# Attention stage: shift products moved ahead of the maxima's products, a turn moved ahead of the output projection

## The chip, the cores and the metric

The kernel runs on one core of a Trainium2 chip. A core has a matrix engine (TensorE, "PE" in the profile, with its weight loads shown apart as "PEld"), VectorE ("DVE"), ScalarE ("ACT"), GpSimd ("POOL") and a queue that issues transfers (SyncE, "SP"). Matrix products land in an accumulator memory (PSUM), which this kernel uses as eight banks, and VectorE or ScalarE read them from there. The metric is the device time of one execution in microseconds: the median of three executions was 3641.82 us (3641.27 to 3644.77).

## The reference, cut to what matters

The input has 16 images of 64 x 64 positions with 128 features. A group normalisation and a two-dimensional recurrence run first, then Nystroem attention over the 4096 tokens of each image (8 heads of 16, 64 landmarks), then a recurrent feed-forward part. The change lies in the attention, of which this is the core:

```
q, k, v = jnp.split(xn @ w_qkv, 3, axis=-1)            # to 8 heads of 16
q_l = q.reshape(b, h, m, l, dh).mean(axis=3)           # 64 landmarks
k_l = k.reshape(b, h, m, l, dh).mean(axis=3)
attn1 = softmax(einsum('bhid,bhjd->bhij', q, k_l))
attn2 = softmax(einsum('bhid,bhjd->bhij', q_l, k_l))
attn3 = softmax(einsum('bhid,bhjd->bhij', q_l, k))
out = attn1 @ moore_penrose_pinv(attn2) @ (attn3 @ v)  # + convolution of v
out = out @ w_out + b_out
```

Both large softmaxes subtract a maximum. In the kernel a maximum is split into three bf16 parts, and a small bf16 product with ones adds the negated maximum into the bank in which the fp32 score products then accumulate; ScalarE takes the exponential from there.

## The kernel before, in words

Attention works on groups of 512 tokens, 8 groups to an image, 128 groups in all. It is a software pipeline over steps: in step `s` the group `new` is projected to keys, values and queries; `mid`, eight steps older (one image back), gets its weights over the landmarks' queries (attn3) and its product with the values; and `first`, `cur`, `third`, `fourth`, `fifth`, `sixth`, some sixteen steps older, go through attn1, the output projection and the feed-forward product. Steps 0 to 7 run `first_step`, 8 to 14 `second_step`, 15 to 127 `step`, and the rest `last_step`. A step that begins an image (`q == 0`, called `start` in the code) also finishes the older image's sums (`gather`, `spread_values`) and makes its shift (`turn_split`).

The order of the work on PE, DVE, ACT and POOL is written out by hand: each engine takes its instructions in the order in which the step calls them. Each name `bank0` to `bank5` and `pair` (two banks) has one buffer, so a new tile of a name waits until the last reader of the tile before it is done.

The parts of a step that the change touches, in order:

- `project_queries` (L997) writes bank 5 with `new`'s queries, and `keep_queries` (L1001) copies them out on ScalarE at L1003.
- `greatest` (L1020) writes the landmark scores of `new` to banks 0 to 3, four row groups of 32 partitions each, and `keep_greatest` (L1026) reduces the four banks to maxima on VectorE, in `step` in the order 3, 2, 1, 0.
- `weigh` (L1048) takes banks 4, 5 and `pair`; it writes the bf16 shift products of `mid` (L1054) and accumulates the fp32 score products (L1060) on them. `weights` (L1066) takes the exponentials on ScalarE, in tile `at_e`, which has one buffer; `add_weights` (L1089) sums them on GpSimd.
- `part_top` (L1143) splits the maxima of `first` on GpSimd, `turn_top` (L1152) turns them on PE into bank 2, and `keep_top` (L1157) copies them out on ScalarE.
- `output` (L1205) projects `third` into bank 3; `keep_sum` (L1210) reads it on VectorE.
- After them come `turn_output` (L970, L960), `attend` (L1175), `convolve`, `divide` (which uses bank 2), `feed` (bank 3, L1238), `turn_rows`, `attend_values`, `soften` and, in the next step, `compare` and the projections.

Of the kernel before, what the change touches and what calls it, by code (L numbers as in the profile page):

```python
# [14 lines left out]
P = 128  # L15
# [830 lines left out]
def attention(nc, tc, t1, gamma, beta, wqkv, ident, mhalf, fixed, xp, rows, qm, km, pinvT, vd, t2, wx, wx_stats, out, ahead):  # L846
# [14 lines left out]
    C = 4  # L861
# [4 lines left out]
    BF = mybir.dt.bfloat16  # L866
    with ExitStack() as ctx:
# [7 lines left out]
        def bank(k, shape, dtype=F32):  # L875
            return ps.tile(shape, dtype, tag=f"bank{k}", name=f"at_bank{k}")

        def banks(*ks):
            return [bank(k, [P, GC]) for k in ks]
# [60 lines left out]
        def carry_factors(gr):  # L940
            gr.nbt = nb = sm.tile([P, 2, C], F32, tag="nb", name="at_nb")
            nc.gpsimd.tensor_tensor(nb[:, 1], gr.T[:, :, F], gr.T[:, :, F + 2], ALU.mult)
            nc.gpsimd.tensor_scalar(nb[:, 0], gr.T[:, :, F + 2], 1.0, None, ALU.add)

        def carry(gr, c, eng):
            x, scale, bias = gr.T[:, c, 0:F], gr.nbt[:, 0, c : c + 1], gr.nbt[:, 1, c : c + 1]
            if eng is nc.scalar:
                nc.scalar.activation(x, x, AF.Identity, bias=bias, scale=scale)
            else:
                eng.tensor_scalar(x, x, scale, bias, ALU.mult, ALU.add)  # L950
# [54 lines left out]
        def turn_split(im):  # L1005
            r = bank(3, [P, P])
            nc.tensor.transpose(r, split.rearrange("p n s -> p (n s)"), ident)
            im.minus = wk.tile([P, P], BF, tag="minus", name="at_minus3")
            nc.scalar.copy(im.minus, r)
# [10 lines left out]
        def greatest(gr):  # L1020

            gr.s = banks(0, 1, 2, 3)
            for n in range(NP):
                nc.tensor.matmul(gr.s[n], gr.im.qm[quarter(n)], gr.KT[quarter(n)], start=True, stop=True)  # L1024
# [20 lines left out]
            im.sums = sm.tile([P, P], F32, tag="sums", name="at_sums")  # L1045
            im.total = wk.tile([P, NP, P], F32, tag="total", name="at_total", bufs=2)

        def weigh(gr, ks=(4, 5)):  # L1048

            both = pair()  # L1050
            s = (*banks(*ks), both[:, 0], both[:, 1])
            im = gr.im
            for n in range(NP):
                nc.tensor.matmul(  # L1054
                    s[n].rearrange("p (c m) -> p c m", c=C), ones_b[n * W2 : n * W2 + 3, :],
                    im.minus[n * W2 : n * W2 + 3, None, :].to_broadcast([3, C, P]), start=True, stop=False,
                )
            for c in range(C):
                for n in range(NP):
                    nc.tensor.matmul(  # L1060
                        s[n][:, c * P : (c + 1) * P], gr.KT[quarter(n), c * P : (c + 1) * P],
                        im.qm[quarter(n)], start=False, stop=(c == C - 1),
                    )
            gr.s = s

        def weights(gr, order=range(NP)):  # L1066
            gr.e = wk.tile([P, NP, C, P], F32, tag="e", name="at_e")
# [75 lines left out]
        def part_top(gr):  # L1143

            gr.top = top = tops[gr.g % 2]
            mx = gr.mx.rearrange("p n c j -> p n j c")
            nc.gpsimd.tensor_copy(top[:, :, 0:2], mx)
            nc.gpsimd.tensor_tensor(mx, mx, top[:, :, 0:2], ALU.subtract)
            nc.gpsimd.tensor_copy(top[:, :, 2:4], mx)
            nc.gpsimd.tensor_tensor(top[:, :, 4:6], mx, top[:, :, 2:4], ALU.subtract)  # L1150

        def turn_top(gr):  # L1152
            gr.pt = bank(2, [P, C, P], BF)
            for c in range(C):
                nc.tensor.transpose(gr.pt[:, c, :], gr.top[:, :, :, c].rearrange("p n s -> p (n s)"), ident_b)

# [74 lines left out]
        def normalise(gr):  # L1231
            gr.z = wk.tile([P, C, F], F32, tag="z", name="at_z")
            for c in range(C):
                nc.scalar.activation(  # L1234
                    gr.z[:, c, :], gr.u[:, c, :], AF.Identity, bias=gr.nb[:, c : c + 1], scale=gr.r3[:, c : c + 1]
                )
# [48 lines left out]
        def second_step(s):  # L1285
            new, after, mid, was = group(s), group(s + 1), group(s - Q), group(s - Q - 1)
            project_keys(new)
            if not was:
                sums(mid.im)
            project_values(new)  # L1290
            if was:
                attend_values(was, 3)
            keep_keys(new)
            keep_projected(new)
            if was:
                keep_values(was)
            turn_rows(after)
            keep_rows(after)
            project_queries(new)
            keep_queries(new)  # L1300
            if not was:
                turn_split(mid.im)
            greatest(new)
            weigh(mid)
            keep_greatest(new, range(NP))
            weights(mid)
            add_weights(mid, (3, 1, 0, 2), mid.g == 0)
            fetch(s)

        def last_step(s):  # L1310
            b, q = divmod(s, Q)
            mid, was = group(s - Q), group(s - Q - 1)
            first, cur, third, fourth, fifth = (group(s - 2 * Q + d) for d in (1, 0, -1, -2, -3))
            start = q == 0
            if s == (B + 1) * Q:
                kvs.close()
            if not cur:
                idle_products(nc, banks(5)[0], ident, wqkv, 384, 384)
                if fourth:
                    normalise(fourth)  # L1320
            if first:
                compare(first)
            if cur:
                softened(cur)
            if start and mid:
                measure_feed(group(s - 2 * Q - 4))
                normalise(fifth)
                turn_output(fifth)
                keep_output(fifth)
                sums(mid.im)  # L1330
                measure(fourth)
                factors(fourth)
                turn_split(mid.im)
            if first:
                topmost(first)
                carry_factors(first)
                carry(first, 2, nc.gpsimd)
            if start and was:
                gather(was.im)
            if first:  # L1340
                part_top(first)
                carry(first, 3, nc.gpsimd)
            if third:
                output(third, 0)
                keep_sum(third)
                measure(third, (0, 1))
            if not cur:
                idle_products(nc, banks(5)[0], ident, wqkv, 384, 384)
            if fifth:
                feed(fifth, 1)  # L1350
            if start and was:
                spread_values(was.im)
            if mid:
                weigh(mid, (2, 3))
                weights(mid, (2, 3, 1, 0))
            if fifth:
                keep_feed(fifth)
            if cur and fourth:
                normalise(fourth)
            if cur:  # L1360
                attend(cur)
            if mid:
                add_weights(mid, (3, 1, 0), mid.g == 0)
            if cur:
                convolve(cur, pair())
                divide(cur, 3)
            if first:
                turn_top(first)
                keep_top(first)
            if cur:  # L1370
                add_convolved(cur)
            if mid:
                attend_values(mid)
                keep_values(mid)
            if fourth:
                turn_output(fourth, 4)
                keep_output(fourth)
            if first:
                carry(first, 0, nc.scalar)
                carry(first, 1, nc.scalar)  # L1380
                soften(first)
            if cur:
                turn_attended(cur)
            if third:
                measure(third, (2, 3))
                factors(third)
            if first:
                carry_bias(first)
            if fifth:
                measure_feed(fifth)  # L1390
            if mid:
                add_weights(mid, (2,), eng=nc.vector)
            fetch(s)
            ahead(s - B * Q)

        def step(s):
# [3 lines left out]
            start = q == 0  # L1400
# [26 lines left out]
                turn_split(mid.im)  # L1427
            if fifth:
                normalise(fifth)
            greatest(new)  # L1430
            if first:
                carry_factors(first)
                carry(first, 2, nc.gpsimd)
            weigh(mid)
            keep_greatest(new)
            if first:
                part_top(first)
            if third:
                output(third)
            weights(mid)  # L1440
            if first:
                carry(first, 3, nc.gpsimd)
            if start and was:
                spread_values(was.im)
            if first:
                turn_top(first)
            if fifth:
                turn_output(fifth)
# [384 lines left out]
```

## Time and profile before

| what | value |
|---|---|
| median of three executions | 3641.82 us |
| the profiled execution, own time | 3638.97 us |
| its span, first to last instruction | 3637.4 us |
| PE, DVE, ACT, POOL busy | 96%, 82%, 69%, 68% of the span |
| first attention steps begin at about | 1615 us |
| a regular step of `step` | 12.77 us |
| a step of `step` that begins an image | 15.79 us |
| steps 10 to 13 (`second_step`) | about 7.55 us |

The page of the profile gives busy time by engine and by group of instructions. A group's row names the line, the engine, the tiles written and read, the shape, the count, the busy time and mean duration, and then the idle time of that engine just before these instructions with what ended it. The timeline lists instructions in order of time: start, duration, engine, line, tiles, count, and in square brackets idle time before and what ended it. "Busy" on PE counts a product until its modelled end, so products that overlap show no gap even where the array waited for a moment. The weight loads have rows of their own. An fp32 product runs as two passes, so eight MATMUL records of L1024 are four products.

### The profile page before, as it was taken

How to read it: one execution, taken by the hardware profiler on the slowest of the kernel's cores; microseconds unless marked ns; L12 is line 12 of the kernel's file. 1: busy time of each engine (PE TensorE's matmuls, PEld its weight loads, DVE VectorE, ACT ScalarE, POOL GpSimd, SP SyncE). 2: the span in 40 equal slices, each digit the busy share in tenths (PEclk: the TensorE clock that was granted, in tenths of full speed). 3: DMA queues.
4: the chain of work that ended last, by engine and by line, in shares of the span. 5: the costliest groups of instructions: out<-in, count | busy, mean ns of one | idle time of the engine just before them, and what ended most of it. 6: DMA issues, size and time to landing. Idle time of an engine off the chain costs nothing. (4 is left out here: it accounts for less than half of the span.)

```text
span 3637.4 us, 99065 instructions
## 1 busy us (share of the span) xinstructions
PE 3503.6 (96%) x36874; PEld 2372.5 (65%) x36874; DVE 2987.7 (82%) x7005; ACT 2499.6 (69%) x5126; POOL 2487.0 (68%) x3843
## 2 busy tenths in 40 slices
PE   7899999999999998999999999999999999997988
PEld 6666665545567666975666666666666666654777
DVE  8699999998889887544888888888888888888665
ACT  0466556666667666345788888888888888876787
POOL 1577877777788885325777777777777777785223
PEclk9999999999999999999999999999999999999999
DMA  9223332333333321033777777777676777667799
GB/s 349 76 75 79 81 84 81 83 83 86 87 86 85 80 77 36 4 74 85 165 174 186 166 165 164 163 167 163 161 162 162 162 166 164 157 143 187 199 273 183
DMA packets 834182, 484.04 MB, mean 133 GB/s; under 512 B 304672, under 2 KB 800672, under 8 KB 833696
## 3 DMA queue, kind: packets, MB, share of 16 engines
q1 hardware_dynamic: 814026, 442.55, 47.7%
q0 software_dynamic: 17728, 34.61, 5.3%
q8 instruction: 294, 4.82, 0.6%
q14 instruction: 192, 1.57, 0.1%
q10 hardware_dynamic: 1942, 0.50, 0.1%
HBM read 239.21 MB, written 238.29 MB: 131 GB/s over the span
## 5 line engine op out<-in xcount | busy, mean ns | idle before, releaser
L1096 POOL TENSOR_TENSOR at_total<-at_total,at_e 128x512 f32<-128x512 f32 x472 | 601.4, 1274 | 238.1 <-ACT at_e L1069 218.5
L290 ACT ACTIVATE ls_g<-ls_z,ls_b 128x304 f32<-128x304 f32 (+26 forms) x950 | 493.4, 545 | 222.8 <-PE ls_z L288 190.8
L283 PE MATMUL ls_z<-ls_xn,ls_w 128*128 128x432 f32 (+28 forms) x1700 | 587.4, 493 | 1.5 <-POOL ls_xn L275 1.2
L283 PEld LDWEIGHTS ls_z<-ls_xn,ls_w 128*128 128x128 f32 x1700 | 310.6, 191 | 189.6 <-issue 98.9
L288 PE MATMUL ls_z<-ls_hsum,ls_u 128*128 128x304 f32 (+26 forms) x1140 | 367.9, 459 | 0.0
L1028 DVE TENSOR_REDUCE at_mxq<-at_bank 128x1 f32<-128x512 f32 x512 | 317.7, 682 | 52.8 <-PE at_bank L1024 52.8
L323 POOL TENSOR_TENSOR ls_tt<-ls_ve,mhalf 128x8 f32<-128x8 f32 (+2 forms) x190 | 312.8, 1646 | 18.3 <-DVE ls_ve L322 2.0
L288 PEld LDWEIGHTS ls_z<-ls_hsum,ls_u 128*128 128x128 f32 x1140 | 210.1, 192 | 128.3 <-issue 78.3
L1173 ACT ACTIVATE at_eT<-at_bank 128x512 f32<-128x512 f32 x512 | 264.3, 603 | 41.4 <-PE at_bank L1168 40.8
L406 ACT ACTIVATE ls_g<-ls_cell 128x304 f32<-128x304 f32 (+26 forms) x190 | 93.2, 491 | 268.4 <-DVE ls_cell L405 268.4
L288 PE MATMUL ls_z<-ls_h,ls_u 128*128 128x304 f32 (+26 forms) x760 | 255.4, 459 | 12.3 <-DVE ls_h L410 12.3
L402 POOL TENSOR_TENSOR ls_g<-ls_g,ls_cell 128x304 f32<-128x304 f32 (+26 forms) x190 | 180.4, 949 | 126.6 <-ACT ls_g L290 115.8
L340 ACT ACTIVATE ls_tt<-ls_tt,ls_nb 128x128 f32<-128x128 f32 (+9 forms) x632 | 261.0, 478 | 4.3 <-POOL ls_tt L323 3.4
L275 POOL TENSOR_TENSOR ls_xn<-ls_xn,grstd 128x272 f32<-128x272 f32 (+40 forms) x186 | 209.8, 1128 | 75.1 <-DVE ls_xn L270 66.7
L1139 DVE TENSOR_REDUCE at_cmx<-at_bank 128x8 f32<-128x512 f32 x256 | 175.5, 685 | 104.0 <-PE at_pair L1131 102.4
L1244 ACT COPY at_fx<-at_bank 128x512 f32<-128x512 f32 x128 | 134.1, 1048 | 143.6 <-PE at_bank L1240 138.0
L1615 DVE SCALAR_TENSOR_TENSOR rc_y<-rc_w,rc_scale,rc_z 128x256 f32<-128x256 f32 x344 | 154.5, 480 | 86.2 <-PE rc_z L1602 84.4
L1234 ACT ACTIVATE at_z<-at_u,at_nb,at_r 128x128 f32<-128x128 f32 x512 | 209.6, 484 | 4.6 <-POOL at_nb L1229 4.5
L288 PEld LDWEIGHTS ls_z<-ls_h,ls_u 128*128 128x128 f32 x760 | 141.1, 191 | 106.8 <-issue 52.5
L1596 POOL DMA_DIRECT2D out_dram<-rc_tt x64 | 77.4, 1209 | 168.2 <-ACT rc_tt L1593 147.8
L1189 DVE STREAM_TRANSPOSE at_t<-at_bank 128x512 f32<-128x512 f32 x256 | 167.9, 694 | 28.4 <-PE at_bank L1180 27.3
L1602 PE MATMUL rc_z<-rc_y,rc_vT 128*128 128x256 f32 x688 | 172.9, 392 | 12.5 <-ACT rc_y L1623 11.8
(283 smaller groups left out, 9809.6 us busy)
## 6 DMA issues: line engine op xcount, KB each, us to landing
at_win<-vd SPq DMA_DIRECT2D x256, 256.0 KB
t<-ls_tt SPq DMA_DIRECT2D x392, 130.0 KB
at_T<-t SPq DMA_DIRECT2D x128, 264.0 KB
gs_xb<-in_x_dram SPq DMA_DIRECT2D x64, 512.0 KB
at_xh<-t SPq DMA_DIRECT2D x128, 256.0 KB
vd<-at_v SPq DMA_DIRECT2D x128, 256.0 KB
t<-at_u SPq DMA_DIRECT2D x128, 256.0 KB
out_dram<-at_u SPq DMA_DIRECT2D x128, 256.0 KB
```

The source lines that it names most:

```text
L275: eng.tensor_tensor(a, a, norm(v, grstd), ALU.mult)
L283: nc.tensor.matmul(v.z[g][:, : v.total], wt[g], v.xn[:, : v.total], start=True, stop=True)
L288: nc.tensor.matmul(view(v, v.first.z[g]), ut[g], hin, start=False, stop=True, skip_group_check=True)
L290: nc.scalar.activation(a[:, : v.cols], z, AF.Tanh if g == 4 else AF.Sigmoid, bias=bt[g])
L323: nc.gpsimd.tensor_tensor(v.tt[:, 0:k, F + 2 : F + 4], ve[:, :, :k].rearrange("p r k -> p k r"), mhalf[:, : 2 * k].rearrange("p (k r) -> p ...
L340: nc.scalar.activation(v.tt[:q, k, F + 4 :], v.tt[:q, k, 0:F], AF.Identity, bias=v.nb[:q, k : k + 1], scale=v.tt[:q, k, F + 3 : F + 4],)
L402: nc.gpsimd.tensor_mul(v.a[1], v.a[1], v.cl)
L1028: nc.vector.tensor_reduce(gr.im.mxq[:, n : n + 1, gr.g], gr.s[n], AX.X, ALU.max)
L1096: eng.tensor_tensor(total, total, e[:, :, c, :], ALU.add)
L1139: nc.vector.tensor_reduce(gr.mx[:, n : n + k].rearrange("p n c j -> p (n c j)"), s.rearrange("p (x m) -> p x m", m=M), AX.X, ALU.max)
L1173: nc.scalar.activation(gr.eT[:, n], gr.s[n], AF.Exp)
L1234: nc.scalar.activation(gr.z[:, c, :], gr.u[:, c, :], AF.Identity, bias=gr.nb[:, c : c + 1], scale=gr.r3[:, c : c + 1])
```

## The change

`weigh` is cut in two. The new `shift_weights` takes the banks and makes the four shift products; `weigh` keeps the score products. In the regular steps of `step`, and in `second_step` from step 9 on, `shift_weights` is called before `greatest` instead of after it, directly behind `project_queries`. Steps that begin an image, and `last_step`, keep the old order. In `step`, `part_top` moves on GpSimd ahead of `carry_factors` and the first `carry`. In the regular steps `turn_top` moves on PE ahead of `output` and takes bank 3, while `output` takes bank 2; steps that begin an image keep order and banks.

```
-        def weigh(gr, ks=(4, 5)):
+        def shift_weights(gr, ks=(4, 5)):
             both = pair()
-            s = (*banks(*ks), both[:, 0], both[:, 1])
+            s = gr.s = (*banks(*ks), both[:, 0], both[:, 1])
             im = gr.im
             for n in range(NP):
                 nc.tensor.matmul(s[n]..., ones_b[...], im.minus[...], start=True, stop=False)
+        def weigh(gr):
+            im, s = gr.im, gr.s
             for c in range(C):
                 for n in range(NP):
                     nc.tensor.matmul(s[n][...], gr.KT[...], im.qm[...], start=False, stop=(c == C - 1))
-            gr.s = s
...
-        def turn_top(gr):
-            gr.pt = bank(2, [P, C, P], BF)
+        def turn_top(gr, k=2):
+            gr.pt = bank(k, [P, C, P], BF)
...
 in second_step:
+            if was:
+                shift_weights(mid)
             greatest(new)
+            if not was:
+                shift_weights(mid)
             weigh(mid)
...
 in last_step:
-                weigh(mid, (2, 3))
+                shift_weights(mid, (2, 3))
+                weigh(mid)
...
 in step:
+            if not start:
+                shift_weights(mid)
             greatest(new)
             if first:
+                part_top(first)
                 carry_factors(first)
                 carry(first, 2, nc.gpsimd)
+            if start:
+                shift_weights(mid)
             weigh(mid)
             keep_greatest(new)
-            if first:
-                part_top(first)
+            if first and not start:
+                turn_top(first, 3)
             if third:
-                output(third)
+                output(third, 3 if start else 2)
             weights(mid)
             if first:
                 carry(first, 3, nc.gpsimd)
             if start and was:
                 spread_values(was.im)
-            if first:
+            if first and start:
                 turn_top(first)
```

## The prediction

> **What bounds the kernel now.** I read the page first (engines, slices, groups), then a table of busy time over two stretches, then the timeline of one regular step on PE, ACT and DVE. From the page:
>
> ```profile
> PE 3503.6 (96%) x36874; PEld 2372.5 (65%) x36874; DVE 2987.7 (82%) x7005; ACT 2499.6 (69%) x5126; POOL 2487.0 (68%) x3843
> L1028 DVE TENSOR_REDUCE at_mxq<-at_bank 128x1 f32<-128x512 f32 x512 | 317.7, 682 | 52.8 <-PE at_bank L1024 52.8
> ```
>
> The 512 reductions are four for each of 128 groups. The table of stretches (length, then busy time and count of PE, PEld, DVE, ACT, POOL, then the granted clock) gives a regular step and one that begins an image:
>
> ```profile
> 1809.86:1822.63 12.77, 12.77 (x188) 8.44 (x187) 11.40 (x26) 10.66 (x21) 10.07 (x18) 1.00 0.97 255
> 1822.63:1838.42 15.79, 15.32 (x214) 11.05 (x213) 12.19 (x28) 11.14 (x23) 12.20 (x27) 1.00 0.65 146
> ```
>
> PE is busy for all 12.77 us; every other engine has over 1 us to spare. So any time in which a product waits lengthens the step, and 98 regular steps (seven in each of 14 images, steps 17 to 127) repeat it. The timeline around the change:
>
> ```profile
> 1809.86 1.02 PE L999 MATMUL at_bank<-at_xT,wqkv 128*128 128x512 f32 x2
> 1810.81 1.14 PE L1024 MATMUL at_bank<-at_KT,qm 32*128 32x512 f32 x8
> 1810.92 0.60 ACT L1003 ACTIVATE at_QT<-at_bank 128x512 f32<-128x512 f32 x1 [0.28 <-PE at_bank L999]
> 1811.78 0.38 PE L1054 MATMUL at_bank<-at_minus,at_onesb 3*128 3x512 bf16 x2
> 1811.99 0.28 PE L1060 MATMUL at_bank<-qm,at_KT 32*128 32x128 f32 x2
> 1812.02 2.48 DVE L1028 TENSOR_REDUCE at_mxq<-at_bank 128x1 f32<-128x512 f32 x4
> 1812.79 0.28 PE L1060 MATMUL at_pair<-qm,at_KT 32*128 32x128 f32 x2
> 1812.99 1.16 PE L1208 MATMUL at_bank<-at_wo,at_oT 128*128 128x128 f32 x8
> 1813.99 0.39 PE L1155 MATMUL at_bank<-at_identb,at_top 128*128 128x128 bf16 x4
> 1814.21 0.61 PE L960 MATMUL at_bank<-ident,at_z 128*128 128x128 f32 x4
> 1814.75 1.09 PE L1180 MATMUL at_bank<-at_eT,at_g 64*32 64x512 f32 x16
> ```
>
> The reader is to see that the queries' projection ends at 1810.88, that ScalarE starts to copy bank 5 at once and is done at 1811.52, and that the shift products, of which the second writes bank 5, start at 1811.78. The maxima's products lie exactly over that copy.
>
> **Part 1, the shift products before the maxima's products.** Nothing is removed: the same four products with the same durations. What moves is their cover. The second shift product needs bank 5, whose last reader is the queries' copy; the built order of the changed kernel lists this wait on ScalarE. The copy cannot start sooner: its idle time of 0.28 us ends with the projection. I need the lag from a ScalarE end to a waiting product. A step that begins an image shows one:
>
> ```profile
> 1829.48 0.25 ACT L1018 COPY at_g<-at_bank 128x64 f32<-128x64 f32 x1
> 1829.78 0.38 PE L1155 MATMUL at_bank<-at_identb,at_top 128*128 128x128 bf16 x4 [0.47 <-ACT at_g L1018]
> 1830.00 0.61 PE L960 MATMUL at_bank<-ident,at_z 128*128 128x128 f32 x4
> ```
>
> 1829.48 + 0.25 to 1829.78 is 0.05. The transposes of L960 behind it, whose data was there, did not pass it; so what stands behind a waiting product on PE waits too. That is `greatest`, and everything after it.
>
> So in the profiled step's own times the second shift product starts at 1811.52 + 0.05 = 1811.57. `greatest` follows 0.21 later (as `weigh` follows now, 1811.78 to 1811.99) at 1811.78. It then takes 0.86 until `weigh`: now 0.97 (1810.81 to 1811.78), of which 0.11 is its first weight load, seen in 1.14 against the 1.03 that the equally shaped L1168 takes when its weights are loaded ahead; behind the shift products the load is hidden. `weigh` starts at 1812.64 instead of 1811.99: **+0.65 us**. The gain that the move could have (a bf16 load instead of an fp32 one at the change from 128 to 32 rows) is at most that 0.11, and it lies inside the wait.
>
> A rule bears on it that the trace of before cannot show, since there the product starts 0.26 after the copy's end. The Trainium skill, "PSUM — Partial Sum Buffer", section "PSUM bank collisions raise a hardware error", says to guard the accumulator by bank, because a product may not write a bank that another engine reads. By the rule Part 1 costs the 0.65; if the write could go beside the read, the part would gain up to 0.11 a step. No run here shows the collision itself.
>
> In `second_step` (steps 9 to 14) I cost this wait at nothing. Its cover is GpSimd: the exponentials wait for the sums of the step before.
>
> ```profile
> 1681.33 1.14 PE L1024 MATMUL at_bank<-at_KT,qm 32*128 32x512 f32 x8
> 1684.32 1.08 ACT L1069 ACTIVATE at_e<-at_bank 128x512 f32<-128x512 f32 x2 [2.29 <-POOL at_total L1096]
> ```
>
> `weigh` ends there 2.26 after `greatest` starts (1810.81 to 1812.79 + 0.28 in the step above), so at 1683.6; the exponentials start 0.7 later, more than 0.65. Without that cover it is 6 x 0.65 = 4 us.
>
> **Part 2, the turn before the output projection, banks 2 and 3 exchanged.** VectorE reduces the four banks of `greatest` in the order 3, 2, 1, 0 and starts when the last product is done. Before, `output` needed bank 3, freed by the first reduction. Now the turn needs that, and `output` needs bank 2, freed by the second. `greatest` ends at 1811.78 + 1.03 = 1812.81 (now 1810.81 + 1.14 = 1811.95; the reductions start 0.07 later, and I take 0.05). Four reductions take 2.48 and one 0.68, so the pitch is 0.60; the first is done at 1812.86 + 0.68 = 1813.54, the second at 1814.14. `weigh`'s last products start at 1812.79 + 0.65 = 1813.44 and the next shape 0.20 later (1812.79 to 1812.99 now), so the turn starts at 1813.64: bank 3 is just free. The turn takes 0.22 (1813.99 to 1814.21). `output` could load at 1813.86 but gets bank 2 at 1814.14 + 0.05 = 1814.19: **+0.33 us**. Bounds: 0 if bank 2 is free in time after all, 0.37 if the lag is 0.07 at both ends; I take the row's own. From `output` to `attend` it is 1.76 now, less the 0.22 of the turn 1.54, so `attend` starts at 1815.73 instead of 1814.75: +0.98 in all.
>
> What is late next: the sum on VectorE starts after the reductions, which end 0.84 later than now, and needs `output`, 0.98 later; both stay under PE's own 0.98. ScalarE's copy of the turned maxima, which `feed` now really waits for in bank 3 (it ended at 1816.20, with `feed` at 1816.20), is behind the exponentials, +0.63, and `turn_output`, +0.98 from 1814.21; it ends near 1816.95, before `feed` at 1817.18. So no third wait, with 0.2 in hand. `part_top` moved on POOL costs nothing: its four operations ended at 1813.01 (L1150, 1812.77 + 0.24), and the turn loads at 1813.64; POOL has 2.7 us a step to spare. The carries behind it wait about 1.1 us longer, which lies in that room; their tile is read on at the end of the step. In the image steps POOL waits for the maxima there, and the carries queue behind that wait instead of ahead of it, with the same room. No transfer moves except by the longer step.
>
> **Sum.** 98 steps x 0.98 = 96.0; step 15, without an output projection, 0.65; the image steps keep their order: 0, though up to 0.2 each (14 x 0.2 = 3) may come back, since GpSimd's shift chain is late by only 0.63 where PE is late by 0.98. Total +97 us on the profiled execution's own 3638.97 (its span is 3637.4): 3736. The median of the three executions lies 2.85 above the profiled one, and the image steps may return about as much, so I let the two cancel and predict **3736 us** (+2.6%). A measurement of this kernel tells 0.2% (7 us) from no change.
>
> **Rivals.**
> - *Only the first wait costs.* If bank 2 is free in time, 99 x 0.65 = 64 us, less up to 98 x 0.05 for the lighter load at the turn: 3698 to 3703. For it speaks that VectorE's lag is read from one row; against it, the second reduction's end is 0.28 after `output` could load. Chance 0.15.
> - *A third wait.* VectorE, 11.40 of 12.77 busy, or bank 3's copy before `feed` falls behind by another 0.2 to 0.4 a step: 98 x 1.2 to 1.4 gives 3757 to 3776. Against it: the step grows by 0.98, so VectorE gains slack. Chance 0.08.
> - *Faster: no wait at either place.* If the queries' copy were over by the time the shift products could start (1810.9), the two lighter loads would gain up to 2 x 0.11 x 98 = 22 us: 3620 at best. The deciding point is the copy's end, 1811.52, 0.6 too late. Chance 0.04. Within 0.2%: 0.01.
>
> **How the numbers follow.** The main case holds 0.72. With Part 2 between its bounds it gives 3703 to 3740. The range joins it to the first rival and stops short of the second: 3697 to 3754, which leaves 0.13 and what the main case misses out. Slower by over 0.2% are the main case and the first two rivals: 0.95; faster 0.04; same 0.01.
>
> **What would show it.** In the changed profile L1054 starts about 0.65 after L999's end with idle time ended by ScalarE's L1003; the output projection's load waits about 0.3 for L1028 on VectorE; a regular step is 13.75 us; `second_step` stays at 7.55 and image steps at 15.6 to 15.8. I am wrong if PE passes the waiting product, if the regular step is under 13.4, or if the wait at the output projection is absent.

## The result, and the profile after

The changed kernel takes 3736.80 us (median of five, 3730.88 to 3741.63) against 3641.82 us (median of five, 3636.52 to 3644.77): a ratio of 1.0259, 95% interval 1.0249 to 1.0270, so it is slower by 95 us. The forecast was 3736. The profiled execution took 3739.7 us, with a span of 3738.2.

On the page of the changed kernel, the engines' row and the maxima's reduction (columns as before: busy time and share; then, behind the bar, busy time, mean ns, and the idle time ahead of the group with what ended most of it):

```profile
PE 3548.2 (95%) x36874; PEld 2392.4 (64%) x36874; DVE 2994.9 (80%) x7005; ACT 2511.2 (67%) x5126; POOL 2497.0 (67%) x3843
L1028 DVE TENSOR_REDUCE at_mxq<-at_bank 128x1 f32<-128x512 f32 x512 | 318.0, 684 | 136.2 <-PE at_bank L1024 136.2
```

The instruction counts are the same as before. PE's busy time grows by 45 us only, because the waits are partly idle time now; VectorE does the same work (2987.7 and 2994.9) but waits 83 us more for the maxima's products (136.2 against 52.8).

The table of stretches for a regular step and for one that begins an image:

```profile
1821.16:1834.93 13.77, 13.25 (x189) 8.73 (x188) 11.53 (x26) 10.77 (x21) 10.09 (x19) 1.00 0.89 223
1834.93:1850.72 15.79, 15.32 (x214) 10.89 (x213) 12.19 (x28) 11.13 (x23) 11.10 (x22) 1.00 0.64 155
```

The regular step grew from 12.77 to 13.77 us, and in it PE has 0.52 us of idle time where it had none; the image step is as long as it was, at the same granted clock of 1.00. Taken over the whole attention stage, from the first queries' product to the last, the time grew from 1563.6 to 1659.0 us, by 95.3. Ahead of that stage the profiled run is 5.8 us longer than the earlier one, in phases that the change does not touch (the stage begins 1614.8 to 1621.5 us into the eight profiled runs of this document, whatever the order in the steps); behind it the two agree within 0.3 us. So the stage itself accounts for the difference of the medians, and the other 5.5 us of the profiled pair do not belong to the change.

The timeline of a regular step shows where the 1.00 us comes from (start, duration, engine, line; in brackets idle time and what ended it):

```profile
1821.16 1.02 PE L999 MATMUL at_bank<-at_xT,wqkv 128*128 128x512 f32 x2
1822.12 0.39 PE L1054 MATMUL at_bank<-at_minus,at_onesb 3*128 3x512 bf16 x1
1822.22 0.60 ACT L1003 ACTIVATE at_QT<-at_bank 128x512 f32<-128x512 f32 x1 [0.27 <-PE at_bank L999]
1822.87 0.37 PE L1054 MATMUL at_bank<-at_minus,at_onesb 3*128 3x512 bf16 x1 [0.37 <-ACT at_QT L1003]
1822.88 0.39 PE L1054 MATMUL at_pair<-at_minus,at_onesb 3*128 3x512 bf16 x2
1822.88 1.25 PE L1024 MATMUL at_bank<-at_KT,qm 32*128 32x512 f32 x8
1824.17 2.48 DVE L1028 TENSOR_REDUCE at_mxq<-at_bank 128x1 f32<-128x512 f32 x4 [0.79 <-PE at_bank L1024]
1824.74 0.28 PE L1063 MATMUL at_pair<-qm,at_KT 32*128 32x128 f32 x2
1824.95 0.41 PE L1157 MATMUL at_bank<-at_identb,at_top 128*128 128x128 bf16 x4
1825.52 0.97 PEld L1210 LDWEIGHTS at_bank<-at_wo,at_oT 128*128 128x128 f32 x8 [0.31 <-DVE at_mxq L1028]
1825.52 1.16 PE L1210 MATMUL at_bank<-at_wo,at_oT 128*128 128x128 f32 x8 [0.15 <-DVE at_mxq L1028]
1826.51 0.60 PE L960 MATMUL at_bank<-ident,at_z 128*128 128x128 f32 x4
1827.04 1.09 PE L1182 MATMUL at_bank<-at_eT,at_g 64*32 64x512 f32 x16
1827.63 0.59 ACT L1161 COPY at_topT<-at_bank 128x512 bf16<-128x512 bf16 x1
1828.49 1.13 PE L1242 MATMUL at_bank<-at_zT,at_wfT 128*128 128x512 f32 x2
```

The first shift product goes straight behind the queries' projection; the second starts 0.75 later, 0.05 after ScalarE's copy of bank 5 ends (1822.22 + 0.60 to 1822.87), and the other two and the maxima's products come with it. The bracket shows 0.37 of idle time, not 0.75, since the first shift product's record, with its modelled end, counts as busy for 0.39. Further down, the turn (L1157) goes where it should, and the output projection (L1210) waits behind it, for the second reduction.

The view of waits of the changed kernel from 1720 to 3100 us, a stretch that holds 85 of the 98 regular steps (engine, tile, line, what released it, then us in total, times, longest):

```profile
DVE at_mxq L1028 <- PE at_bank L1024: 81.0, 98, 2.3
PE at_bank L1054 <- ACT at_QT L1003: 31.3, 85, 0.4
PEld at_bank L1210 <- DVE at_mxq L1028: 26.7, 85, 0.3
PE at_bank L1210 <- DVE at_mxq L1028: 13.3, 85, 0.2
```

For the kernel before, the same view from 1720 to 3000 us has no wait of L1054 for L1003, three short waits (0.6 us in all) of the output projection's load for L1028, and 13.5 us in the first row. These are the two waits that the prediction named, in every one of the 85 steps.

`second_step` shows the cover at work: the same first wait is there, and the step is as long as before.

```profile
1688.40 0.37 PE L1054 MATMUL at_bank<-at_minus,at_onesb 3*128 3x512 bf16 x1 [0.31 <-ACT at_QT L1003]
1690.27 0.27 PE L1063 MATMUL at_pair<-qm,at_KT 32*128 32x128 f32 x2
1690.64 1.08 ACT L1071 ACTIVATE at_e<-at_bank 128x512 f32<-128x512 f32 x2 [2.30 <-POOL at_total L1098]
```

The last score product ends at 1690.54, and the exponentials, which GpSimd releases, start 0.10 later. Steps 10 to 13 stay at 7.55 us.

### The profile page after: what moved, and what is told of

Its sections match the earlier page's. It is cut to its first block, busy times and chain, and to the rows that moved or that the text cites. A ratio compares the mean times of both kernels' runs of the same rounds, so it can differ in the third digit from the quotient of the medians.

```text
span 3738.2 us, 98969 instructions
## 1 busy us (share of the span) xinstructions
PE 3548.2 (95%) x36874; PEld 2392.4 (64%) x36874; DVE 2994.9 (80%) x7005; ACT 2511.2 (67%) x5126; POOL 2497.0 (67%) x3843
## 5 line engine op out<-in xcount | busy, mean ns | idle before, releaser
L1028 DVE TENSOR_REDUCE at_mxq<-at_bank 128x1 f32<-128x512 f32 x512 | 318.0, 684 | 136.2 <-PE at_bank L1024 136.2
L1071 ACT ACTIVATE at_e<-at_bank 128x512 f32<-128x512 f32 x256 | 139.0, 595 | 100.8 <-PE at_pair L1063 72.1
```

What stands on the lines that cost most here:

```text
L1028: nc.vector.tensor_reduce(gr.im.mxq[:, n : n + 1, gr.g], gr.s[n], AX.X, ALU.max)
```

## Experiments

The theory to be tested: the loss is two waits on PE, each for an accumulator bank, and nothing else; 0.65 us a regular step for bank 5, held by the queries' copy, and 0.33 for bank 2, held until the second reduction. Rivals are that moving the products itself costs (more changes between kinds of product, or maxima that reach VectorE later), that the second wait belongs to another cause, and that one of the two parts is worth keeping by itself. All kernels below compute the full result. In the comparisons the kernel before was run again beside them: median 3640.62 us for the first four, 3641.78 for the last two.

Some readings below are medians over the regular steps of a trace, of times after the start of the second of the two passes of the queries' projection. They are put together here, in us:

| | before | after | e1 | e2 | e3 | e7 | e5 |
|---|---|---|---|---|---|---|---|
| maxima's products end | 1.66 | 2.53 | 2.53 | 1.66 | 1.78 | 1.78 | 2.53 |
| last score product starts | 2.50 | 3.15 | 3.15 | 2.50 | 2.50 | 2.50 | 3.15 |
| turn of the maxima starts | 3.70 | 3.36 | 4.35 | 2.71 | 3.70 | 2.70 | 3.91 |
| output projection starts | 2.70 | 3.93 | 3.35 | 3.07 | 2.70 | 3.20 | 4.13 |
| `attend` starts | 4.46 | 5.45 | 5.17 | 4.60 | 4.46 | 4.73 | 5.61 |
| regular step | 12.77 | 13.77 | 13.49 | 12.92 | 12.77 | 13.04 | 13.92 |

### e1: the shift products alone

The changed kernel with the turn and the output projection put back in order and banks. (GpSimd's earlier `part_top` stays.)

```
-            if first and not start:
-                turn_top(first, 3)
             if third:
-                output(third, 3 if start else 2)
+                output(third)
...
-            if first and start:
+            if first:
                 turn_top(first)
```

> Only the shift products are moved; output projection, turn and their banks as before (GpSimd's earlier split of the maxima stays). Theory: the second shift product waits for the queries' copy out of bank 5 and holds all of PE behind it, 0.65 us a regular step, and the second wait is absent, since the output projection needs only the first reduction: step 13.42 us, time about 3706 us. Rival, one cost of 1.0 us a step that comes from the shift products' place alone (VectorE late behind the later maxima): step 13.77, about 3737 us.

Measured: 3708.22 us (3704.88 to 3711.11), ratio 1.0188 (1.0172 to 1.0203), +67.6 us; regular step 13.49. The timeline of e1:

```profile
1816.57 0.38 PE L1054 MATMUL at_bank<-at_minus,at_onesb 3*128 3x512 bf16 x1
1817.32 0.37 PE L1054 MATMUL at_bank<-at_minus,at_onesb 3*128 3x512 bf16 x1 [0.37 <-ACT at_QT L1003]
1817.33 1.25 PE L1024 MATMUL at_bank<-at_KT,qm 32*128 32x512 f32 x8
1818.62 2.48 DVE L1028 TENSOR_REDUCE at_mxq<-at_bank 128x1 f32<-128x512 f32 x4 [0.79 <-PE at_bank L1024]
1819.40 1.16 PE L1210 MATMUL at_bank<-at_wo,at_oT 128*128 128x128 f32 x8
1820.39 0.39 PE L1157 MATMUL at_bank<-at_identb,at_top 128*128 128x128 bf16 x4
1820.63 0.42 PEld L960 LDWEIGHTS at_bank<-ident,at_z 128*128 128x128 f32 x4
1820.66 0.63 PE L960 MATMUL at_bank<-ident,at_z 128*128 128x128 f32 x4
```

The wait for the copy is whole, and the output projection follows the scores without a wait; the rival that put the whole loss on the shift products' place (13.77 us a step) falls. By the table, the last score product and the output projection are 0.65 later than before, as worked out; but the step is longer by 0.715, and that further 0.065 appears between the turn and `attend`. It is a third, small wait, for bank 1: the turn of the output (L960) writes it, and the third reduction holds it until about 1820.50 (1818.62 + 0.68 + 2 x 0.60). The view of waits does not list it, being under 0.15 us, but the times show it. In the median of the regular steps the first weight load of L960 starts 0.12 after the third reduction's end in e1 and again in e4 below, although the turn ahead of it comes 0.02 sooner in e4. (Of the 0.12, 0.05 is an instruction on PE's queue that only waits for VectorE's semaphore.) In e1 the load so stands 0.07 behind the start of the turn's last product. In the kernel before the load starts 0.25 after the reduction's end and less than 0.01 behind that product, so nothing waits there. In the changed kernel, where everything there is later still, this piece is absent.

### e2: the turn alone

The shift products go back behind the maxima's products, in `step` and in `second_step`; Part 2 stays.

```
-            if not start:
-                shift_weights(mid)
             greatest(new)
...
-            if start:
-                shift_weights(mid)
+            shift_weights(mid)
             weigh(mid)
```

> Only the turn is moved ahead of the output projection and the banks 2 and 3 are exchanged; shift products as before, behind the maxima's products. Theory: the second reduction ends at 1813.30 in the times of the step before, the output projection's load could start at 1813.2, so it waits about 0.1 and the step grows by 0.1 to 0.15 us: 12.9 us, about 3655 us. The 0.33 of the prediction needs the shift's delay. Rival, the exchange costs its 0.33 by itself: step 13.1, about 3674 us. Rival, lighter load gains: step 12.72, about 3637 us.

Measured: 3654.71 us (3651.97 to 3658.06), ratio 1.0036 (1.0023 to 1.0049), +14.1 us; regular step 12.92, +0.14. The timeline of e2:

```profile
1817.55 1.14 PE L1024 MATMUL at_bank<-at_KT,qm 32*128 32x512 f32 x8
1818.76 2.48 DVE L1028 TENSOR_REDUCE at_mxq<-at_bank 128x1 f32<-128x512 f32 x4
1819.73 0.41 PE L1157 MATMUL at_bank<-at_identb,at_top 128*128 128x128 bf16 x4
1820.10 1.16 PE L1210 MATMUL at_bank<-at_wo,at_oT 128*128 128x128 f32 x8
```

The turn takes 0.22 when nothing waits; the output projection starts 0.37 after it, so it waits 0.15, until 0.06 after the second reduction's end (1818.76 + 0.68 + 0.60 = 1820.04). Part 2 loses by itself too. The two parts alone sum to 67.6 + 14.1 = 82 us, not 95: the second wait is 0.15 here and 0.35 in the changed kernel. What differs is when the maxima's products end, 0.87 later there, while the score products, behind which the turn stands, end only 0.65 later. That difference of 0.22 accounts for the larger wait (0.15 + 0.22 = 0.37, against 0.35). So the wait grows by 0.20 a step; e1's own 0.065, which the changed kernel does not have, is set against it, and the 0.14 that is left makes the 13 us between 82 and 95.

### e3: the product to bank 5 left behind

e1, but only three shift products (banks 4 and the pair) go ahead of the maxima's products in regular steps; the one to bank 5 follows them. `second_step` keeps the old order.

```
-            if not start:
-                shift_weights(mid)
+            if not start:
+                both = pair()
+                mid.s = (bank(4, [P, GC]), None, both[:, 0], both[:, 1])
+                shift_products(mid, (0, 2, 3))
             greatest(new)
+            if not start:
+                mid.s = (mid.s[0], bank(5, [P, GC]), mid.s[2], mid.s[3])
+                shift_products(mid, (1,))
```

> As e1_shift_alone, but the shift product that writes bank 5 stands behind the maxima's products, the other three ahead of them; second_step as before. Theory: no product waits for the queries' copy, so the 0.65 goes and the lighter load at the change of shape gains about 0.05: step 12.7 to 12.77 us, 3636 to 3642 us, same as before or just faster. Rival, any shift product ahead of the maxima's products costs (VectorE gets them 0.2 later): step 12.95 or more, 3660 us or more.

Measured: 3640.25 us (3634.69 to 3645.15), ratio 0.9997 (0.9988 to 1.0006), no difference; regular step 12.77. The timeline of e3 (the shift products are L1057):

```profile
1810.89 0.39 PE L1057 MATMUL at_bank<-at_minus,at_onesb 3*128 3x512 bf16 x1
1810.89 0.39 PE L1057 MATMUL at_pair<-at_minus,at_onesb 3*128 3x512 bf16 x2
1810.90 1.24 PE L1024 MATMUL at_bank<-at_KT,qm 32*128 32x512 f32 x8
1811.87 0.38 PE L1057 MATMUL at_bank<-at_minus,at_onesb 3*128 3x512 bf16 x1
1811.98 0.27 PE L1066 MATMUL at_bank<-qm,at_KT 32*128 32x128 f32 x1
1812.76 0.27 PE L1066 MATMUL at_pair<-qm,at_KT 32*128 32x128 f32 x2
1812.87 0.27 PE L1066 MATMUL at_bank<-qm,at_KT 32*128 32x128 f32 x1
```

Moving the three products costs nothing, nor does GpSimd's earlier `part_top`, which is in this kernel too; waiting for bank 5 is the cost of Part 1. The move brings nothing either. The gain that the prediction bounded at 0.11 a step, from a bf16 weight load at the change from 128 to 32 rows, does not reach the step: the last score product starts at 2.50 as before. The trace shows where it stays. The last score product to the pair starts 0.11 sooner than before (median 2.40 against 2.50), and of the two single banks one is 0.09 sooner (2.39 against 2.48); but the other still has its last product at 2.50 (2.49 before). The bank served last is bank 5's by the order of issue, since the rows do not number the banks: its row group still begins with an fp32 load. The output projection comes after the last of the four, so the three that are ahead gain nothing for the step. (In the changed kernel, where all four begin with a shift product, the second shift product starts 0.76 later than the maxima's products did before, and the last score product only 0.65 later: there the 0.11 comes back, behind the wait.)

### e4: the waiting product last of the four

e1 with the four shift products issued in the order 0, 2, 3, 1, all ahead of the maxima's products, so that the one to bank 5 comes last.

```
-                shift_weights(mid)
+                shift_weights(mid, order=(0, 2, 3, 1))
             greatest(new)
```

> As e1_shift_alone, but the four shift products are ordered banks 4, pair, pair, 5, all ahead of the maxima's products. Theory: three go at once, the last still waits for the copy and the maxima's products stand behind it: 0.65 us a step as in e1_shift_alone, about 3706 us (within 0.1 a step, 10 us). Rival, products of other row groups pass a waiting one: step below 13.0, under 3665 us.

Measured: 3706.73 us (3705.31 to 3708.94), ratio 1.0183 (1.0167 to 1.0198); regular step 13.49, as e1. The timeline of e4:

```profile
1815.46 0.38 PE L1057 MATMUL at_bank<-at_minus,at_onesb 3*128 3x512 bf16 x1
1815.46 0.39 PE L1057 MATMUL at_pair<-at_minus,at_onesb 3*128 3x512 bf16 x2
1816.21 0.37 PE L1057 MATMUL at_bank<-at_minus,at_onesb 3*128 3x512 bf16 x1 [0.36 <-ACT at_QT L1003]
1816.21 1.23 PE L1024 MATMUL at_bank<-at_KT,qm 32*128 32x512 f32 x8
```

Now three shift products are issued before the wait, and still the maxima's products, none of which uses bank 5, start only with the fourth. In regular steps e3 and e4 differ by where one small product stands, ahead of or behind work that does not need its bank, and by 0.72 us, 66 us in all (the order in `second_step` differs too, which is worth the 0.5 us named below): a product that waits holds all that stands behind it on PE.

### e7: both parts, without the first wait

e3 with Part 2 as in the changed kernel. It asks whether the size of the second wait follows the end of the maxima's products: that is 0.11 later here than in e2, while the score products end at the same time.

```
             keep_greatest(new)
+            if first and not start:
+                turn_top(first, 3)
             if third:
-                output(third)
+                output(third, 3 if start else 2)
...
-            if first:
+            if first and start:
                 turn_top(first)
```

> Both parts of the change, with the shift product to bank 5 left behind the maxima's products (the other three ahead), so the first wait is gone and Part 2 stays whole. Theory (Part 2's wait is set by when the maxima's products end, and they end 0.13 us later here than in the kernel before because of the three products ahead): the turn's exchange alone cost 0.14 a step, here 0.14 + 0.13 = 0.27: a regular step of 13.02 to 13.06 us, 3664 to 3669 us. Rival (Part 2 costs a fixed 0.14 and the rest of its 0.34 in the changed kernel belongs to something else): 12.91 us, 3654 us.

Measured: 3666.60 us (3664.39 to 3668.11), ratio 1.0072 (1.0055 to 1.0089); regular step 13.04, +0.27. The timeline of e7 (the turn is L1160, the output projection L1213):

```profile
1819.34 2.48 DVE L1028 TENSOR_REDUCE at_mxq<-at_bank 128x1 f32<-128x512 f32 x4
1820.18 0.41 PE L1160 MATMUL at_bank<-at_identb,at_top 128*128 128x128 bf16 x4
1820.68 0.97 PEld L1213 LDWEIGHTS at_bank<-at_wo,at_oT 128*128 128x128 f32 x8 [0.24 <-DVE at_mxq L1028]
```

The second reduction ends at 1819.34 + 0.68 + 0.60 = 1820.62 and the load starts 0.06 later. So Part 2 has no price of its own: its wait is 0.15 in e2, 0.28 here and 0.35 in the changed kernel (from the turn's start to the output projection's in the table, less the turn's 0.22), and it goes by how late the reductions begin against the last score product: 0.77 ahead of its start in e2, 0.64 here, 0.57 in the changed kernel. (The changed kernel's step is only 0.28 above e1's, 13.77 less 13.49, because e1 has 0.065 of its own.) The rival of a fixed 0.14 (3654 us) falls. It also shows that e3's three products ahead, free by themselves, make the maxima 0.11 to 0.13 later, which only Part 2 notices.

### e5: the two reductions exchanged

The changed kernel with VectorE reducing bank 2 first and bank 3 second in regular steps.

```
-            keep_greatest(new)
+            keep_greatest(new, (3, 2, 1, 0) if start else (2, 3, 1, 0))
```

> The changed kernel with one thing different: in regular steps VectorE reduces the four banks in the order 2, 3, 1, 0, so bank 2 comes free with the first reduction and bank 3 with the second. Theory (the order of VectorE's reductions decides what waits on PE): now the output projection's bank is free early and the turn waits for bank 3, to about 3.91 us after the queries' last pass starts instead of 3.36; the output projection follows 0.22 later, at 4.13 instead of 3.93. A regular step of 13.93 to 13.97 us instead of 13.77, about 3752 to 3757 us; the wait for L1028 moves from L1210 to the turn. Rival (the output projection's 0.33 has another cause than bank 2): the output projection stays where it is, 13.77 us, 3737 us; or it is freed, 13.5 us, 3710 us.

Measured: 3750.91 us (3749.48 to 3754.20), ratio 1.0302 (1.0285 to 1.0319), +14 us on the changed kernel; regular step 13.92. The timeline of e5:

```profile
1826.66 2.49 DVE L1028 TENSOR_REDUCE at_mxq<-at_bank 128x1 f32<-128x512 f32 x4 [0.77 <-PE at_bank L1024]
1828.00 0.39 PE L1157 MATMUL at_bank<-at_identb,at_top 128*128 128x128 bf16 x4 [0.48 <-DVE at_mxq L1028]
1828.17 0.97 PEld L1210 LDWEIGHTS at_bank<-at_wo,at_oT 128*128 128x128 f32 x8
1828.22 1.11 PE L1210 MATMUL at_bank<-at_wo,at_oT 128*128 128x128 f32 x8
```

The wait for L1028 has moved from the output projection to the turn, and the output projection follows the turn without one. That is the mechanism of Part 2 shown from the other side: whichever comes second in VectorE's order is what PE waits for. The step is 0.01 to 0.05 under what was expected and the time 1 us under its lower end: the output projection starts 0.20 later, as expected, but its first load now runs beside the turn (it takes 1.11 instead of 1.16), which gives back 0.05.

## Why the prediction was right

**Both waits, by its own steps.** Its times, put on the start of the queries' projection (the row of L999), against the step shown above:

| event | predicted | measured |
|---|---|---|
| second shift product starts | 1.71 | 1.71 |
| maxima's products start | 1.92 | 1.72 |
| maxima's products end | 2.95 | 2.97 |
| first score product starts | 2.78 | 2.68 |
| turn of the maxima starts | 3.78 | 3.79 |
| output projection starts | 4.33 | 4.36 |
| `attend` starts | 5.87 | 5.88 |
| ScalarE's copy of the turned maxima ends | 7.09 | 7.06 |
| `feed` starts | 7.32 | 7.33 |
| regular step | 13.75 | 13.77 |

Part 1's 0.65 is met (last score product 2.50 to 3.15), and Part 2's 0.33 came out at 0.34 of the step. Between them one piece of the working is off: the prediction let the maxima's products start 0.21 behind the second shift product and last 1.03, while their record starts 0.01 behind it and lasts 1.25. The two differences cancel, so the end, on which all that follows rests, is right to 0.02. The lag of 0.05 us from an engine's end to a waiting product, read from one row of an image step, holds at the second shift product (0.05) and roughly at the output projection's load (the second reduction ends at 1824.17 + 0.68 + 0.60 = 1825.45, the load starts at 1825.52: 0.07; 0.05 in the median of the regular steps). That the waiting product holds what stands behind it, the assumption on which all of Part 1 rests, is shown by e3 against e4.

**No third wait.** ScalarE's copy of the turned maxima ends 0.27 before `feed`, where 0.2 was expected, and from `attend` to `feed` it is 1.45 us in both kernels. The rival of a third wait is out for the changed kernel. The rival of only the first wait is out by e1, which has that wait alone and loses 67.6 us instead of 95. (e1 has a small third wait of its own, 0.065 for bank 1.) The rival of a gain is out by the end of the copy, at which the second shift product starts.

**What was costed at nothing.** `second_step` is covered by GpSimd as worked out, with 0.10 us left of the cover where 0.05 was expected. The earlier `part_top` costs nothing that e3 can show. Only the interval out of step 9, the first with the new order, grew, by 0.54.

**Small misses.** The image steps were allowed to return up to 0.2 each and returned nothing: 15.79 both times. Step 15 was costed at +0.65; the two intervals in which `second_step` hands over to `step` changed by -1.61 and +0.55. The first of these does not follow the order of the products: e3 and e7, with the old order in `second_step`, have 11.3 us as the changed kernel, e1 and e4 do, while e5, with the new one, has the 12.9 of the kernel before (and e2, with the old one, 14.2). What sets it was not followed up. The second is about +0.5 in e3 and e7 too, where no product waits for bank 5, so it can't be put down to that wait alone. The sum over the stage is 95.8 (97 regular steps) + 0.54 - 1.06 = 95.3 us.

**What was luck.** That 3736 met the median of 3736.80 to within 1 us is luck in part. The five runs of the changed kernel lie between 3730.88 and 3741.63, the -1.61 is in the measured pair and not in the prediction, and the prediction let the 2.85 us between the median and the profiled run cancel against a gain in the image steps that did not come. What carries the forecast is the regular step, 13.75 against 13.77, and the two waits in it.

**The terms interact.** The prediction worked the second wait out behind the first, from the late end of the maxima's products, and not as a price for an edit alone. e1 and e2 show why that matters: the parts alone cost 67.6 and 14.1 us, together 95.

**What stays open.** By the rule of the Trainium skill that the prediction named ("PSUM — Partial Sum Buffer", section "PSUM bank collisions raise a hardware error") Part 1 costs its 0.65, and that is what it costs. The runs show that the product starts 0.05 us after the copy's end and not earlier, which is how the kernel is built to wait; what a write beside the read would do was not tried, so the rule itself is not tested here. The two intervals at the start of `step`, -1.61 and +0.55, have no shown cause.

## What to carry to other kernels

Before an instruction is moved up on an in-order engine, look up the last reader of the bank that it writes and when that reader ends: work that stands between a projection and its copy may look idle for the mover, yet it is the cover of the copy, and one product that loses its cover holds everything behind it. If three of four products are free to go and one is not, splitting them (e3) removes the loss, but look whether the step gains at all before paying for the split. When two tiles exchange buffers, compare the order in which their readers let go with the order in which the writers come; and price parts of a change in sequence, since a wait's size depends on what is late ahead of it.

## What was not expected of the hardware

The shift products and the maxima's products of one step use four row groups, and records of both start within 0.01 us of each other (L1054 at 1822.88, L1024 at 1822.88), though in program order all shift products stand ahead. Yet in e4 the same maxima's products did not start beside a shift product that waited, 0.75 us long. So products on different row groups run beside each other once issued, but a wait is taken in program order for all of them. The idle bracket on PE undercounts such a wait: 0.37 us is shown between two products that start 0.75 us apart (1822.12 and 1822.87), because the record of the first, with its modelled end, covers the rest.
